# Butterfly weights regrouped between two rounds: trips through DRAM replaced by TensorE transposes, in a decoder block on one Trainium2 core

## The chip, the core and the metric

The kernel runs on one core of a Trainium2 chip (trn2). The metric is the device time of one execution in microseconds (us). TensorE (PE in the profile) multiplies matrices and writes into PSUM; VectorE (DVE), ScalarE (ACT) and GpSimd (POOL) do the element-wise work and empty PSUM; SyncE (SP) issues the DMA transfers. All data are fp32, and every fp32 matmul appears in the trace as two records; a transpose appears as one.

## The reference

Input x has 4 tokens, 2048 batch positions and 512 features. Three residual steps follow one another, each behind a layer norm: a diagonal state-space recurrence along the tokens, a cross-attention with 16 heads over 77 context rows, and a feed-forward net whose hidden layer of 2048 passes through butterfly transforms.

```python
x = x + recurrence(layernorm(x))
x = x + cross_attention(layernorm(x), ctx)
h = layernorm(x) @ W_exp + b_exp              # 512 -> 2048
h = butterfly(h, up_weights)                  # 11 stages
h = gelu(h + up_bias)
h = butterfly(h, down_weights)                # 11 stages
x = x + (h @ W_con + b_con) + down_bias       # 2048 -> 512

def butterfly(y, weights):                    # stage s mixes i with i + 2**s
    for s in range(11):
        yr = y.reshape(*lead, nb, 2, 2 ** s)
        a, b = yr[..., 0, :], yr[..., 1, :]
        w = weights[s]                        # a 2x2 matrix for each pair
        y = stack([w00 * a + w01 * b, w10 * a + w11 * b])
```

## The kernel before, in words

The rows of x are worked in 16 units, each of 128 positions with their 4 tokens. For a unit, `front` does the recurrence, the attention and the last layer norm, and `feed_forward` the rest. `feed_forward` of unit u runs interleaved with `front` of unit u + 1: after every few matmuls, its `step` takes one piece of the other's work. Dense products are done with seven half-size products instead of eight (`seven`, `up`, `down`), so the weights are needed in seven pieces: `up7`, `wq7` and `dn7` in DRAM, `wo` in SBUF.

The butterflies are linear, so an opening (`_prepare`) multiplies them into W_exp and W_con once, on the chip, and the units use dense weights. The 11 stages go in two rounds. The low 7 stages mix only inside blocks of 128 rows: 16 blocks, each a full 128 x 128 matrix `e`, made by `_low_products` from the coefficients (`low_up`, `low_dn`, 2 MB each) in six element-wise steps, each twice as long as the one before. The high 4 stages mix rows that are 128 apart. With the rows regrouped, so that row 16p + m lies on partition p in group m, they are 16 matrices of 128 x 128 in which only 16 diagonals are filled; `diagonal` spreads the products `hp` over a mask to make one such `bd`.

Between the rounds the weights must change from the one order of rows to the other:

- Up: 16 matmuls L258 (512 columns), evictions L230 (ACT) and L232 (DVE) in turn, 16 stores to `rows_up`, four loads back in the other order, then 64 matmuls L283 (128 columns) with `bd`. The bias goes the same way by L259, `brow` and L284.
- Down: 16 matmuls L314 with `bd`, 16 stores to `rows_dn`, four loads back, then 16 matmuls L325 with `e`.

`bd` is made on POOL (L236), as are both sets of low products (L174). SP issues its transfers one after the other; one that stands behind a transfer that must wait waits too.

The opening of the program as a whole: `_recurrence_taps` computes the recurrence's matrices (L111 to L124); `_keys_values` makes keys and values of the context (L147, L156), from tiles that lie in the room of `wup`; then `front(0)` (normalizing L428 and transposes L439, recurrence L469, layer norm L375 to L401 with transposes L410, queries L454, scores L512, softmax L516 to L522, transposed scores L534, outputs L544, output projection L454 with `sw`/`ot`) is taken in turn with the pieces of `_prepare`, one piece of the one for one of the other. Sums of weight blocks (L301 to L304 for up7, L334 to L341 for dn7) come at the end of each half. PSUM banks for `_prepare` rotate among three tags (`banks`). The scheduler orders the instructions of each engine; the first matmul of unit 0's feed-forward is the first L613.

Of the kernel before, what the change touches and what calls it, by code (L numbers as in the profile page):

```python
# [17 lines left out]
P = 128  # L18
# [115 lines left out]
def _keys_values(nc, psum, ctx_t, wk_t, wv_t, kbd, vsb, room):  # L134


    wk = room[:, 0, :].rearrange("p (c e) -> p c e", c=NC)
    wv = room[:, 1, :].rearrange("p (c e) -> p c e", c=NC)
    ct = room[:, 2, 0 : NC * T * NK].rearrange("p (c k) -> p c k", c=NC)
# [3 lines left out]
    nc.gpsimd.memset(kbd, 0.0)  # L143
# [9 lines left out]
    for b in range(T):  # L153
        ps = psum.tile([P, 512], F32, tag="b", name="ps_v")
        for c in range(NC):
            nc.tensor.matmul(ps[0:NK, :], lhsT=ct[:, c, b * NK : (b + 1) * NK], rhs=wv[:, c, :],  # L156
                             start=c == 0, stop=c == NC - 1)
        nc.scalar.copy(vsb[:, b, :], ps[0:NK, :])


def _low_products(nc, low, transposed):


    e, off = low[:, 0 : 2 * NB], 2 * NB
    for s in range(1, LOW):
        n = 2 ** s
        w = low[:, off : off + NB * 2 * n]
        off += NB * 2 * n
        if transposed:
            v, old = w.rearrange("p (x c) -> p x c", c=2), e.unsqueeze(2).to_broadcast([P, NB * n, 2])  # L170
        else:
            v = w.rearrange("p (b r x) -> p b r x", b=NB, r=2)
            old = e.rearrange("p (b x) -> p b x", b=NB).unsqueeze(2).to_broadcast([P, NB, 2, n])
        nc.gpsimd.tensor_tensor(v, v, old, ALU.mult)  # L174
        e = w
    return e.rearrange("p (b x) -> p b x", b=NB)
# [28 lines left out]
def _regrouped(nc, pool, scratch, e, name):  # L205

    nc.sync.dma_start(out=scratch.rearrange("(b j) k -> j b k", j=P), in_=e)
    out = pool.tile([P, NB, NB], F32, tag="hp", bufs=2, name=name)
    nc.sync.dma_start(out=out, in_=scratch.rearrange("(p m) k -> p m k", m=NB))
    return out  # L210


def _prepare(nc, pool, banks, dram, ident, wexp_t, up_low, up_high, up_bias, dn_low, dn_high, wcon, wup, wdn, bias,
# [4 lines left out]

    sub = P // NB
    rows = dram.tile([HID, D], F32, name="rows_up")  # L220
    rows_dn = dram.tile([HID, D], F32, name="rows_dn")
    brow = dram.tile([2, HID], F32, name="brow")
    hscr = [dram.tile([HID, NB], F32, name=f"hscr{i}") for i in range(2)]
    t = wdn
    mask = pool.tile([P, sub], F32, name="mask")
    nc.vector.tensor_reduce(mask, ident.rearrange("p (b i) -> p i b", i=sub), AX.X, ALU.add)

    def evict(i, out, ps):
        if i % 2:
            nc.scalar.copy(out, ps)  # L230
        else:
            nc.vector.tensor_copy(out, ps)  # L232

    def diagonal(hp, m):
        bd = pool.tile([P, NB, sub], F32, tag="bd", bufs=3, name="bd")
        nc.gpsimd.tensor_tensor(bd, hp[:, m, :].unsqueeze(2).to_broadcast([P, NB, sub]),  # L236
                                mask.unsqueeze(1).to_broadcast([P, NB, sub]), ALU.mult)
        return bd.rearrange("p b i -> p (b i)")

    low = pool.tile([P, NB * 2 * (P - 1)], F32, tag="lowc", name="low_up")  # L240
    high = pool.tile([P, HIGH, NB // 2, 4], F32, tag="highc", bufs=2, name="high_up")
    b1 = pool.tile([P, NB], F32, name="b1")
    b2 = pool.tile([P, NB], F32, name="b2")
    nc.sync.dma_start(out=low, in_=up_low)
    nc.sync.dma_start(out=high, in_=up_high)
    nc.sync.dma_start(out=bias, in_=up_bias)
    src = wexp_t.rearrange("(b p) d -> p b d", p=P)
    nc.sync.dma_start(out=b1, in_=src[:, :, D])
    for i in range(4):
        nc.sync.dma_start(out=t[:, 4 * i : 4 * i + 4, :], in_=src[:, 4 * i : 4 * i + 4, 0:D])  # L250
    yield
    e = _low_products(nc, low, False)
    hp = _regrouped(nc, pool, hscr[0], _high_products(nc, pool, high, False), "hp_up")
    yield
    pb = banks()
    for b in range(NB):
        ps = banks()
        nc.tensor.matmul(ps, lhsT=e[:, b, :], rhs=t[:, b, :], start=True, stop=True)  # L258
        nc.tensor.matmul(pb[:, b : b + 1], lhsT=e[:, b, :], rhs=b1[:, b : b + 1], start=True, stop=True)  # L259
        evict(b, t[:, b, :], ps)  # L260
        nc.sync.dma_start(out=rows[b * P : (b + 1) * P, :], in_=t[:, b, :])
        if b % 4 == 3:
            yield
    nc.vector.tensor_copy(b1, pb[:, 0:NB])
    nc.sync.dma_start(out=brow[0, :].rearrange("(b p) -> p b", p=P), in_=b1)
    nc.sync.dma_start(out=b2, in_=brow[0, :].rearrange("(p m) -> p m", m=NB))
    back = rows.rearrange("(p m) d -> p m d", m=NB)
    for i in range(4):
        nc.sync.dma_start(out=t[:, 4 * i : 4 * i + 4, :], in_=back[:, 4 * i : 4 * i + 4, :])
    high = pool.tile([P, HIGH, NB // 2, 4], F32, tag="highc", bufs=2, name="high_dn")  # L270
    nc.sync.dma_start(out=high, in_=dn_high)
    yield
    hp_dn = _regrouped(nc, pool, hscr[1], _high_products(nc, pool, high, True), "hp_dn")
    low = pool.tile([P, NB * 2 * (P - 1)], F32, tag="lowc", name="low_dn")
    nc.sync.dma_start(out=low, in_=dn_low)
    e = _low_products(nc, low, True)
    yield
    pb = banks()
    for m in range(NB):
        bd = diagonal(hp, m)  # L280
        ps = banks().rearrange("p (c k) -> p c k", c=NC)
        for c in range(NC):
            nc.tensor.matmul(ps[:, c, :], lhsT=t[:, m, c * P : (c + 1) * P], rhs=bd, start=True, stop=True)  # L283
        nc.tensor.matmul(pb[:, m : m + 1], lhsT=bd, rhs=b2[:, m : m + 1], start=True, stop=True)  # L284
        evict(m, wup.rearrange("p c (k m) -> p m c k", m=NB)[:, m], ps)
        if m % 4 == 3:
            yield
    nc.vector.tensor_copy(b2, pb[:, 0:NB])
    nc.sync.dma_start(out=brow[1, :].rearrange("(p m) -> p m", m=NB), in_=b2)
    nc.sync.dma_start(out=b1, in_=brow[1, :].rearrange("(b p) -> p b", p=P))  # L290
    nc.vector.tensor_tensor(bias, b1, bias, ALU.add)
    h, k = HID // 2, NC // 2
    for p in range(NB // 2):
# [4 lines left out]
        for i, a in enumerate((a11, a12, a22)):  # L298
            nc.sync.dma_start(out=up7[p][:, i], in_=a)
        s = pool.tile([P, 4, k, P], F32, tag="s", bufs=1, name="s")  # L300
# [3 lines left out]
        nc.vector.tensor_tensor(s[:, 3], a12, s[:, 1], ALU.subtract)  # L304
        nc.sync.dma_start(out=up7[p][:, 3:7], in_=s)
        if p % 2:
            yield
    src = wcon.rearrange("(p m) d -> p m d", m=NB)
    for i in range(4):
        nc.sync.dma_start(out=t[:, 4 * i : 4 * i + 4, :], in_=src[:, 4 * i : 4 * i + 4, :])  # L310
    yield
    for m in range(NB):
        ps = banks()
        nc.tensor.matmul(ps, lhsT=diagonal(hp_dn, m), rhs=t[:, m, :], start=True, stop=True)  # L314
        evict(m, t[:, m, :], ps)
        nc.sync.dma_start(out=rows_dn.rearrange("(p m) d -> p m d", m=NB)[:, m, :], in_=t[:, m, :])
        if m % 4 == 3:
            yield
    src = rows_dn.rearrange("(b p) d -> p b d", p=P)
    for i in range(4):  # L320
        nc.sync.dma_start(out=t[:, 4 * i : 4 * i + 4, :], in_=src[:, 4 * i : 4 * i + 4, :])
    yield
    for b in range(NB):
        ps = banks()
        nc.tensor.matmul(ps, lhsT=e[:, b, :], rhs=t[:, b, :], start=True, stop=True)  # L325
        evict(b, wdn[:, b, :], ps)
        if b % 4 == 3:
            yield
    h = NB // 2
    b11, b12, b21, b22 = (wdn[:, r * h : r * h + h, c * (D // 2) : (c + 1) * (D // 2)] for r in range(2) for c in range(2))  # L330
    t1, t2, t3, n4 = (wup[:, i, :].rearrange("p (b d) -> p b d", b=h) for i in range(4))
    for i, w in ((0, b11), (1, b21), (2, b22)):
        nc.sync.dma_start(out=dn7[i], in_=w)
    nc.vector.tensor_tensor(t1, b12, b11, ALU.subtract)  # L334
    nc.sync.dma_start(out=dn7[4], in_=t1)
    nc.gpsimd.tensor_tensor(t3, b22, b12, ALU.subtract)
    nc.sync.dma_start(out=dn7[6], in_=t3)
    nc.vector.tensor_tensor(t2, b22, t1, ALU.subtract)
    nc.sync.dma_start(out=dn7[5], in_=t2)
    nc.vector.tensor_tensor(n4, b21, t2, ALU.subtract)  # L340
    nc.sync.dma_start(out=dn7[3], in_=n4)  # L341
# [4 lines left out]
def kernel(ctx: ExitStack, tc: tile.TileContext, x, ctx_t, ssm_vec, ssm_vt, ssm_vinv, wq_t, wk_t, wv_t,  # L346
# [16 lines left out]
    make_identity(nc, ident)  # L363

    def load_x(u):
        xt = (xlast if u % 3 == 2 else xpool).tile([P, T, D], F32, tag=f"xt{u % 3}", name=f"xt{u}")
        nc.sync.dma_start(out=xt, in_=x[:, u * P : (u + 1) * P, :].rearrange("t p d -> p t d"))
# [91 lines left out]
    def front(u, xt, res, wq=None):  # L459
# [18 lines left out]
        if wq is None:  # L478
            wq = work.tile([P, 7, NC // 2, D // 2], F32, tag="pt", bufs=1, name="wq")
            nc.sync.dma_start(out=wq, in_=wq7)  # L480
# [108 lines left out]
    def feed_forward(u, xt, rhs, other):  # L589
# [70 lines left out]
        for p in range(h):  # L660
# [3 lines left out]
            up_mid(p)  # L664
            r, d = xt[:, p // 2, p % 2 * (D // 2) : (p % 2 + 1) * (D // 2)], slice(p % 2 * (D // 2), (p % 2 + 1) * (D // 2))
# [58 lines left out]
    xts = {0: load_x(0)}  # L724
    ready = []
    with tc.tile_pool(name="prep", bufs=1) as pool:
        wup = pool.tile([P, NC, HID], F32, name="wup")
        wdn = pool.tile([P, NB, D], F32, name="wdn")
        _recurrence_taps(nc, pool, psum, ssm_vec, ssm_vt, ssm_vinv, gt)
        prep = _prepare(nc, pool, banks, dram, ident, wexp_t, up_low, up_high, up_bias, dn_low, dn_high, wcon,  # L730
                        wup, wdn, hbias, up7, dn7)
        next(prep)
        _keys_values(nc, psum, ctx_t, wk_t, wv_t, kbd, vsb, wup)
        wq = work.tile([P, 7, NC // 2, D // 2], F32, tag="pt", bufs=1, name="wq")
        src = wq_t.rearrange("(c p) e -> p c e", p=P)
# [104 lines left out]
```

## Time and profile before

| | |
|---|---|
| median of 3 runs | 2663.07 us (2663.07 to 2663.37) |
| profiled execution | 2661.34 us |
| its span | 2659.6 us |
| mean granted TensorE clock | 0.989 of full speed |
| PE, DVE, POOL, ACT busy over the span | 96%, 54%, 36%, 30% |
| first L613 matmul (end of the opening) | 246.58 us after the span's start |
| PE, DVE, POOL, ACT busy in 0 to 246.6 | 176.72, 135.06, 102.84, 47.44 us |
| HBM read, written | 306.00, 41.96 MB |

All views come from one profiled execution, whose time is 1.73 us under the median. An engine's busy time counts its instructions, not what it waits for. A row of groups reads: line, engine, operation, output and inputs, shapes, number of records, then busy time in us, the mean of one record in ns, and the idle time ahead of them with what ended it. A row of the chain gives start and length in us, engine, tile and line. A row of the windows gives the stretch in us, its length, and the busy time of each engine in it.

### The profile page before, as it was taken

To read this page: it belongs to the slowest core of one execution; us is meant where nothing else is said; L and a number is where in the kernel's file an instruction comes from. 1 tells how busy PE (TensorE), PEld (TensorE's weight loads), DVE (VectorE), ACT (ScalarE), POOL (GpSimd) and SP (SyncE) were. 2 spreads that over 40 slices of the span, in tenths; PEclk is the share of its full clock that TensorE was granted. 3 is DMA by queue.
4 is the path that set the end of the run, shared out by engine and by line. 5 is a ranking of instruction groups with operands and counts; after the bars stand their busy time and mean duration, and the time that the engine had idled before them with its cause. 6 is when DMAs were issued, how large, how long until landed. Compare 5 with 4: busy or idle time off the path is not lost.

```text
span 2659.6 us, 36812 instructions
## 1 busy us (share of the span) xinstructions
PE 2565.1 (96%) x14216; PEld 2157.9 (81%) x14216; DVE 1439.1 (54%) x3308; ACT 793.6 (30%) x1440; POOL 965.7 (36%) x1054
## 2 busy tenths in 40 slices
PE   6787999999999999999999999999999999999999
PEld 3545888888888888888888888888888888888888
DVE  4366554565465455546555555645555564554541
ACT  1222413324141332414133341413234241423420
POOL 5343351523334152433415243342524234252523
PEclk9898999999999999999999999999999999999999
DMA  7575233342423334342333333233343324333243
GB/s 265 187 253 210 104 123 124 111 145 97 144 102 131 119 115 137 116 138 93 134 113 127 125 121 133 105 133 107 121 138 112 138 96 145 105 127 108 96 130 139
DMA packets 100158, 350.34 MB, mean 132 GB/s; under 512 B 17936, under 2 KB 46736, under 8 KB 81808
## 3 DMA queue, kind: packets, MB, share of 16 engines
q1 hardware_dynamic: 99984, 347.98, 37.9%
q8 instruction: 113, 1.85, 0.3%
q14 instruction: 61, 0.50, 0.1%
HBM read 306.00 MB, written 41.96 MB: 131 GB/s over the span
## 4 chain that ended last, share of the span: by engine, by line
PE 85%; DVE 6%; ACT 5%; DMA 2%; POOL 1%; issue 1%; SPq 0%; ACTq 0%; DVEq 0%; POOLq 0%
PE ps_a L678 13%; PE ps_b L613 10%; PE ps_b L678 8%; PE ps_w L454 7%; PE ps_q L454 7%; PE ps_c L613 7%; PE ps_a L613 7%; PE ps_c L678 6%; PE ps_sc L512 5%; PE ps_pt L534 4%; PE ps_s L469 3%; PE ps_o L544 2%; PE ps_t L410 2%; ACT L518 1%; ACT L618 1%; DVE st L375 1%
## 5 line engine op out<-in xcount | busy, mean ns | idle before, releaser
L613 PE MATMUL ps_b<-tb,w_up 128*128 128x256 f32 x1536 | 396.7, 379 | 0.0
L678 PE MATMUL ps_a<-w_dn,a 128*128 128x256 f32 x1536 | 373.0, 380 | 0.0
L656 POOL TENSOR_TENSOR s<-a,a 128x256 f32<-128x256 f32 x128 | 93.1, 727 | 675.3 <-ACT a L618 452.8
L613 PEld LDWEIGHTS ps_b<-tb,w_up 128*128 128x128 f32 x1536 | 287.1, 190 | 39.5 <-DVE tb L585 0.4
L678 PEld LDWEIGHTS ps_a<-w_dn,a 128*128 128x128 f32 x1536 | 282.4, 190 | 41.6 <-issue 3.0
L618 ACT ACTIVATE a<-a,hbias 128x256 f32<-128x256 f32 x384 | 193.7, 508 | 408.7 <-DVE a L651 277.6
L613 PE MATMUL ps_a<-xnt,w_up 128*128 128x256 f32 x1024 | 263.9, 380 | 0.0
L678 PE MATMUL ps_c<-w_dn,s 128*128 128x256 f32 x1024 | 248.6, 379 | 0.0
L411 ACT COPY xnt<-ps_t 128x512 f32<-128x512 f32 x128 | 73.6, 587 | 546.5 <-PE ps_t L410 546.5
L522 POOL TENSOR_TENSOR pr<-pr,sm 128x1232 f32<-128x1232 f32 x64 | 144.0, 2249 | 248.7 <-DVE sm L521 242.4
L613 PEld LDWEIGHTS ps_a<-xnt,w_up 128*128 128x128 f32 x1024 | 191.9, 191 | 25.7
L678 PEld LDWEIGHTS ps_c<-w_dn,s 128*128 128x128 f32 x1024 | 188.7, 190 | 27.8
L666 POOL TENSOR_TENSOR xt<-xt,ybias 128x256 f32<-128x256 f32 x128 | 99.9, 813 | 236.9 <-DVE xn L401 236.9
L562 DVE TENSOR_TENSOR xt<-ps_w,xt 128x512 f32<-128x512 f32 x96 | 66.1, 689 | 213.3 <-PE ps_w L454 144.2
L512 PE MATMUL ps_sc<-kbd,qt 128*128 128x308 f32 x512 | 176.6, 442 | 5.1 <-DVE pr L517 3.5
L534 PE MATMUL ps_pt<-ident,pr 128*77 128x128 f32 x1024 | 145.3, 277 | 14.2 <-DVE pt L539 5.7
L534 PEld LDWEIGHTS ps_pt<-ident,pr 128*77 128x77 f32 x1024 | 117.9, 148 | 49.1 <-ACT a L618 11.0
L454 PE MATMUL ps_q<-xnt,wq 128*128 128x256 f32 x640 | 153.2, 382 | 2.1 <-DVE qt L491 1.4
L518 ACT ACTIVATE pr<-pr 128x308 f32<-128x308 f32 x256 | 111.5, 457 | 137.1 <-DVE pr L517 136.6
L454 PEld LDWEIGHTS ps_q<-xnt,wq 128*128 128x128 f32 x640 | 122.1, 191 | 20.2 <-DVE qt L491 1.8
L613 PE MATMUL ps_c<-tb,w_up 128*128 128x256 f32 x512 | 131.7, 379 | 0.4 <-DVE tb L583 0.4
L613 PE MATMUL ps_c<-xnt,w_up 128*128 128x256 f32 x512 | 131.5, 379 | 0.0
(196 smaller groups left out, 4461.6 us busy)
## 6 DMA issues: line engine op xcount, KB each, us to landing
w_up<-up SPq DMA_DIRECT2D x128, 896.0 KB, 4.6
w_dn<-dn SPq DMA_DIRECT2D x112, 1024.0 KB, 4.8
wq<-wq SPq DMA_DIRECT2D x16, 1792.0 KB, 7.6
xt<-in_x SPq DMA_DIRECT2D x16, 1024.0 KB, 5.5
out<-xt SPq DMA_DIRECT2D x64, 256.0 KB, 4.8
wdn<-in_wexp_t SPq DMA_DIRECT2D x4, 1024.0 KB, 10.7
rows_up<-wdn SPq DMA_DIRECT2D x16, 256.0 KB, 2.9
wdn<-rows_up SPq DMA_DIRECT2D x4, 1024.0 KB, 12.5
```

Source lines behind the costliest of these rows:

```text
L411: nc.scalar.copy(xnt[:, :, t, :], ps)
L454: nc.tensor.matmul(tiles[key][:, r, :], lhsT=lhs(i, r, k), rhs=rhs(i, r, k), start=key == i and r == 0 and k == 0, stop=k == 1, skip_group ...
L469: nc.tensor.matmul(ps[:, 2 * i : T, f * NS : (f + 1) * NS], lhsT=xpt[:, i, c * (P // NS) + f, :], rhs=gt[:, 0 : T - 2 * i, :], start=i == ...
L512: nc.tensor.matmul(ps[:, 0 : 4 * NK], lhsT=qt[:, g, t, :], rhs=kbd[:, t, g, :], start=True, stop=True)
L518: nc.scalar.activation(pg, pg, AF.Exp, scale=1.0 / math.sqrt(DH))
L522: nc.gpsimd.tensor_tensor(pr, pr, sm.unsqueeze(2).to_broadcast([P, NH, NK]), ALU.mult)
L534: nc.tensor.transpose(pt_ps[0:NK, j, :], pr[:, 4 * g + j, :], ident)
L613: nc.tensor.matmul(ps, lhsT=w[:, c, :], rhs=rhs[i - 1][:, c], start=first and c == 0, stop=c == 1, skip_group_check=True)
L618: nc.scalar.activation(out, x, AF.Gelu, bias=hbias[:, b : b + 1])
L656: nc.gpsimd.tensor_tensor(s1, a21, a22, ALU.add)
L666: nc.gpsimd.tensor_tensor(r, r, ybias[:, d], ALU.add)
L678: nc.tensor.matmul(ps[:, t, :], lhsT=act[p][lhs[i]][:, t, :], rhs=w[:, p, :], start=first and p == 0 and t == 0, stop=p == h - 1, skip_gro ...
```

## The change

What it does, in the changed file's lines:

- *Up.* The first round is turned over: 64 matmuls L276 of 128 columns with `wdn` (that is, w_exp) as the stationary operand and `e` as the moving one, so that the features lie on partitions. The evictions write them into `mid` (the room of `wup`), grouped by m. 64 transposes L285, four to an eviction, bring group m to `t`. Then 64 matmuls L298 with `bd`: four groups m share a PSUM bank, each writing every fourth column.
- *Down.* The second round comes first as before, as 64 matmuls L333 in the same manner as L298, then 64 transposes L343, then 16 matmuls L352 with `e`, in an order that lets the stores of `dn7` go in two halves.
- `bd` is made on DVE. Evictions go 3 to ACT and 2 to DVE of every five. The last of the low_up products is shared by DVE and POOL, and its load is in two parts. The bias matmuls L267 come ahead of the others. `s` has two buffers.
- The order: coefficients and w_exp are loaded first, x after them; the keys and values come behind the up weights, from tiles of their own; the products of low_dn come after the sums of the up weights; `ybias` is summed at the very end; the load of x for unit u + 2 comes after the second p in `feed_forward`. Some instructions are held to the program's order (`keep_in_program_order`, `keep`).

The core of the diff of `_prepare`:

```diff
-    for b in range(NB):
-        ps = banks()
-        nc.tensor.matmul(ps, lhsT=e[:, b, :], rhs=t[:, b, :], start=True, stop=True)
-        nc.tensor.matmul(pb[:, b : b + 1], lhsT=e[:, b, :], rhs=b1[:, b : b + 1], start=True, stop=True)
-        evict(b, t[:, b, :], ps)
-        nc.sync.dma_start(out=rows[b * P : (b + 1) * P, :], in_=t[:, b, :])
...
-    back = rows.rearrange("(p m) d -> p m d", m=NB)
-    for i in range(4):
-        nc.sync.dma_start(out=t[:, 4 * i : 4 * i + 4, :], in_=back[:, 4 * i : 4 * i + 4, :])
...
+    mid = wup.rearrange("p c (m k) -> p c m k", m=NB)
+    for g in range(4):
+        for c in range(NC):
+            ps = banks()
+            for j in range(4):
+                b = 4 * g + j
+                nc.tensor.matmul(ps[:, j * P : (j + 1) * P], lhsT=t[:, b, c * P : (c + 1) * P],      # L276
+                                 rhs=e[:, b, :], start=j == 0, stop=True, skip_group_check=True)
+            evict(mid[:, c, :, 32 * g : 32 * g + 32].rearrange("p m k -> p k m"), ps.rearrange("p (k m) -> p k m", m=NB))
...
+    for m in range(NB):
+        ps = banks()
+        for c in range(NC):
+            nc.tensor.transpose(ps[:, c * P : (c + 1) * P], mid[:, c, m, :], ident)                  # L285
+        evict(t[:, m, :], ps)
...
+    for g in range(4):
+        bd = [diagonal(hp, 4 * g + j) for j in range(4)]
+        for c in range(NC):
+            ps = banks()
+            for j in range(4):
+                nc.tensor.matmul(ps.rearrange("p (k m) -> p m k", m=4)[:, j], lhsT=t[:, 4 * g + j, c * P : (c + 1) * P],  # L298
+                                 rhs=bd[j], start=j == 0, stop=True, skip_group_check=True)
+            evict(wup[:, c, :].rearrange("p (k m) -> p k m", m=NB)[:, :, 4 * g : 4 * g + 4], ps.rearrange("p (k m) -> p k m", m=4))
...
-        nc.sync.dma_start(out=rows_dn.rearrange("(p m) d -> p m d", m=NB)[:, m, :], in_=t[:, m, :])
...
+    def turned(b):
+        ps = banks()
+        for c in range(NC):
+            nc.tensor.transpose(ps[:, c * P : (c + 1) * P], wup[:, c, b * P : (b + 1) * P], ident)  # L343
+        evict(t[:, b, :], ps)
```

In the whole program, `prep` is taken five pieces ahead of `front(0)`, and the weights of the queries are loaded after its first pieces:

```diff
-        for _ in prep:
-            next(first, None)
+        for _ in range(5):
+            next(prep)
...
+        for n, _ in enumerate(prep):
+            for _ in range(1 + (n > 8)):
+                next(first, None)
+            if n == 7:
+                next(keys)
```

## The prediction

> **What bounds the kernel now.** I read the busy windows first, then the chain of waits, then the groups by shape. The columns of the windows are stretch, length, busy time of PE, weight loads, DVE, ACT and POOL (instruction records in brackets), granted PE clock, DMA share, GB/s.
>
> ```profile
> 0.00:246.60 246.60, 176.72 (x809) 114.17 (x810) 135.06 (x312) 47.44 (x77) 102.84 (x161) 0.89 0.71 243
> 400.00:550.00 150.00, 148.67 (x847) 127.01 (x847) 83.74 (x197) 48.41 (x88) 53.62 (x56) 1.00 0.34 118
> 84.00:90.74 6.74, 0.06 (x2) 0.01 (x1) 6.16 (x24) 0.00 (x0) 0.00 (x0) 0.83 0.82 190
> 90.74:94.35 3.61, 3.61 (x17) 3.00 (x17) 1.49 (x3) 1.76 (x3) 0.00 (x0) 0.50 0.90 53
> 154.61:219.65 65.04, 49.44 (x266) 26.00 (x267) 49.45 (x75) 17.74 (x34) 22.11 (x14) 0.86 0.79 294
> ```
>
> After the opening TensorE is busy for 148.67 of 150 us, so nothing but TensorE work counts there. The opening ends at 246.58, with the first L613 matmul of unit 0; in it PE is idle for about 70 us. In the built programs the PE rows from that matmul on are the same one by one, and so are ACT's; DVE, POOL and SP differ by the bias add and the x load only. So the opening alone can change the time. What it waits for stands in the chain (start, length, who):
>
> ```profile
> 3.16 8.62 DMA low_up<-in_up_low
> ...
> 22.20 4.46 POOL low_up L174
> 26.70 2.08 PE ps_p L258 x2
> ...
> 57.52 13.73 PE ps_v L156 x32
> ...
> 88.03 17.89 DMA low_dn<-in_dn_low
> ...
> 181.62 3.13 DMA rows_dn<-wdn
> ...
> 185.35 9.40 DMA wdn<-rows_dn
> ...
> 194.80 10.57 PE ps_p L325 x24
> ```
>
> Two DRAM trips stand in it. The up weights are stored, and their reload keeps the queue full (DMA share 0.90) while low_dn comes in; the down weights are stored and reloaded between 181.62 and 194.80, 13.2 us. One matmul of 512 columns is two records, so L156 gives 13.73 / 16 = 0.858 at full clock, and 0.2145 for 128 columns.
>
> ```profile
> L283 PE MATMUL ps_p<-bd,wdn 128*128 128x128 f32 x128 | 18.3, 295 | 0.0
> L232 DVE COPY wdn<-ps_p 128x512 f32<-128x512 f32 x24 | 16.3, 687 | 34.4 <-PE ps_p L258 26.7 <-PE ps_p L325 4.1 <-PE ps_p L314 3.4
> L230 ACT COPY wdn<-ps_p 128x512 f32<-128x512 f32 x24 | 14.1, 586 | 47.1 <-PE ps_p L258 27.0 <-PE ps_p L314 10.7 <-PE ps_p L325 9.4
> L232 DVE COPY wup<-ps_p 128x512 f32<-128x512 f32 x8 | 8.3, 1037 | 12.8 <-PE ps_p L283 12.8
> ```
>
> A contiguous eviction takes 0.69 on DVE and 0.59 on ACT; one whose writes are 64 bytes apart, 1.04 on DVE (its ACT twin 1.035).
>
> **The change step by step.** New lines are those of the changed file. Each step gets the time at which it ends.
>
> *First round.* The load of low_up is split, so the six products on POOL start with the first half, and the longest, 4.46 on POOL, is shared: half of it is 2.3 on POOL. low_up lands at 11.8 before; half of its 2 MB, first in the queue, should be there near 7. The products before the last sum to 0.32 + 0.45 + 0.73 + 1.22 + 2.29 = 5.0, and the high products no longer sit among them (3.15 + 1.49 + 0.56 = 5.2 out of the path). So the matmuls start at 7 + 5.0 + 2.3, some 15 instead of 26.7 (bounds 13, and 20 if the second half or w_exp lands late). The 16 one-column bias matmuls L267 now stand ahead, partly at low clock: 5.5, to 20.5. The same work as before, now 64 matmuls L276, 64 x 0.2145 = 13.7, with about 4 of recurrence among them: 38.4. Its 16 strided evictions, 16 x 1.04 on two engines = 8.3, hide beside it.
>
> *Transposes of the up weights.* 64 of L285 replace the trip. In the 3.61 us row 16 of them took 0.226 each at clock 0.50, so 0.113 at full clock: 7.2 of PE. Sixteen evictions, 7 x 0.69 on DVE and 9 x 0.59 on ACT, lie beside the normalizing of unit 0 (L428, 0.71 each, on DVE), so evictions set the stage: 9.8 with it, 1.4 for the eviction ahead and 0.7 for the first diagonal block: 50.3.
>
> A rule speaks against these stretches: the Trainium skill, TensorE: Matmul & The Clock Gate, section Part 4: PE-mode transpose, says that transposes do not count as busy for the clock gate. Its row here shows 0.50, but after 6.7 us with nothing on PE, which leaves rule and idleness apart as causes. If the clock stayed at 0.50 through a stretch, 64 x 0.226 = 14.5 would replace 9.8; I take 3 us for both stretches together (bounds 0 and 6.4, the clock row on either side).
>
> *Second round, up.* The 64 matmuls L298 are those of L283, 18.3 there; recurrence sums 3.3 and waits behind DVE, which shares a lock with POOL's wq products, 2.4: 74.3. That such a lock is there: a DVE subtraction of 2048 columns took 2.28 alone and 5.99 while POOL did one, which took 6.97. Diagonal blocks leave POOL, 32 x 0.43, for DVE, where an operation twice as wide took 0.42; I take 0.26. Waiting in that place for brow (9.9 before, PE behind a 7.0 us load) goes: b2 is fetched under the transposes.
>
> *Keys, values.* 8.55 + 13.73 in the chain plus 1.3 of L498: 97.8. Beside them lie the sums s and the up7 stores, which cost some 5.5 us each pair in the chain before (3.28 of it a store that the single s buffer waited on); with two buffers I take 3 each, 8 in 23 us, done with the matmuls. Were that cover gone, it would cost up to 5.
>
> *Statistics.* Before, PE stood 6.7 us (84.00 to 90.74) while DVE did the layer norm of unit 0; that stays, 7.6 with 0.9 of eviction: 105.4. Then 16 transposes cold, 3.6, and the first queries, 8.7: 117.7.
>
> *Down weights.* On POOL the products of low_dn (10 us) now stand behind s and before the query sums; the first four diagonal blocks share DVE with them, 4.3: 122. The remaining queries and three groups of L333 take 18.3: 140.3. Then attention and L343, L352. DVE carries it: maxima 7.6, subtractions 7.5, sums 5.7 + 1.0, transposed scores out 5.4, outputs 2.8, blocks 1.1, evictions 10, t1, t2, n4 as halves 6.9 = 48.0; 8 for the lock and 5 for waits on PE give 61, to 201.3 (bounds 50 and 70; the stage from 154.61 to 219.65 was 65.0 with 49.45 on DVE and both trips' end in it).
>
> *Tail.* From the last attention output 27.4 before (219.65 to 246.58 and its issue). The eight additions L666 on POOL, 0.79 each, leave this place; beside them the last Newton steps took 0.65 instead of 0.2, so 2.4 go: 25, to 226.3. SP also carries fourteen half stores of dn7 instead of seven, but they start with the first half, some 15 us earlier; a store lands in 5 and w_up in 4.6, by about 219. A new wait: the fourth operand n4 of unit 0 stands on POOL behind the bias add, which waits for the down-bias load; ready 5.8 after the first L613 and needed at 9.4. If that cover went, the excess is paid once. The load of wq at the start of a unit and that of x two units on are in new places on SP; w_up passes both, and wq has 38.4 - 19.5 - 7.6 = 11.3 us to spare (issue, landing and first use within a unit).
>
> *Sum.* 246.6 - 226.3 = 20.3, less 3 for the clock: 17.3. Profiled time: 2661.3 - 17.3 = 2644.0 (its span of 2659.6 and 1.7 around it). The median of the runs lies 1.7 above the profiled execution, so 2663.1 - 17.3 = 2645.8, rounded to 2646.
>
> **Rivals.** *Strided writes into PSUM slow TensorE.* L298 and L333, 128 matmuls, write every fourth column. No row of before does that: the nearest, L469, writes blocks of 64 columns and runs at 0.43 for 256, the contiguous rate. As L283 goes at 0.2145 when warm, writes that double it add 128 x 0.2145 = 27.5, and the kernel is 10 slower, 2673. It decides from 17.3 / 128 = 0.135 more for each matmul. Below zero it can't go, since the columns are the same. I take nothing, the nearest row's value. The Trainium skill, Advanced Engine Details and Errata, section Memory Cachelines, speaks for it: any PSUM pattern that isn't contiguous slows matmuls significantly. It gives no figure; no row here agrees or differs yet.
>
> *One wait for another.* The fixed order lets PE stand at POOL's low_dn products, the statistics and SP's stores for as long as it stood at the trips: the last stage at its 70 and 8 more at the blocks, gain about 0 (-5 to 5), 2663. For it: DVE and POOL are as full as before in the stage from 154.61, 49.45 of 65. Against it: the trip of 13.2 is in the chain, and no work takes its place.
>
> *The early start counts in full.* With the late stage at 50 instead of 61, the gain is 28 to 33, 2632. Against it: 48.0 of DVE work leaves 2 us for all waits.
>
> That the change doesn't do what it says is excluded: the built program has 128 more transposes and no row stores.
>
> **How the numbers follow.** A measurement here tells 0.2%, 5.3 us. Forecast, a gain of 5.3 to 31: 0.74; over 31: 0.08; about nothing: 0.08, of which 0.07 within 5.3; strided writes, slower by over 5.3: 0.10. Slower comes to 0.11, faster to 0.82. The unknown ends of the steps add as squares, 5, 4, 9 and 2.4 one way, 11 and 2 the other: gain 6 to 28. Reaching for eight in ten across the cases I take a gain of 1 to 33: 2630 to 2662, which holds the forecast's 0.74 and some 0.07 of its neighbours.
>
> **What would show it.** In the profile after: the first L276 near 15 to 20 us; L298 and L333 near 18 us for 128 records (36 would be the rival); the stretch of L285 near 10 at a clock above 0.8; PE waiting about 7 for DVE at the statistics; the first L613 at 226 to 230; and windows past it unchanged at 148.67 of 150. A first L613 beyond 245, or a steady window with less PE, makes the prediction wrong.

## The result and the profile after

The changed kernel takes 2661.61 us (median of 12 runs, 2659.90 to 2666.95), the kernel before 2663.07 (12 runs, 2660.91 to 2664.74). The ratio is 0.9997, 95% interval 0.9989 to 1.0006: no change, where 2646 was forecast.

The profiled execution took 2664.3 us, 2.7 above the median of its kernel and 3.0 above the one before. Its windows, with the columns of before (stretch, length, busy time of PE, weight loads, DVE, ACT, POOL, granted PE clock, DMA share, GB/s):

```profile
0.00:248.90 248.90, 195.05 (x1128) 152.99 (x1129) 157.71 (x352) 61.62 (x103) 81.28 (x122) 0.93 0.51 165
400.00:550.00 150.00, 148.67 (x846) 127.00 (x845) 82.36 (x195) 47.79 (x87) 53.34 (x56) 1.00 0.35 125
20.80:47.60 26.80, 26.77 (x111) 23.17 (x111) 6.08 (x18) 3.51 (x4) 11.51 (x64) 1.00 0.79 201
160.46:217.97 57.51, 50.49 (x354) 33.68 (x352) 47.80 (x76) 24.32 (x47) 13.93 (x6) 0.94 0.22 78
```

The steady part is as it was, 148.67 of 150. The first L613 of before (the matmul is L642 now) starts at 248.96 instead of 246.58, so 2.4 of the 2.9 us by which this execution's span is longer lie in the opening. PE is idle there for 53.9 us instead of 69.9, since the trips are gone, but it is busy for 18 us more: new work, and old work done slowly. The third row is the surprise: PE is idle for only 0.03 of 26.8 us, and yet the first round is late. The timeline of PE over it and behind (start, length, line, tile, records, idle time ahead):

```profile
20.83 6.99 PE L267 MATMUL ps_p<-b,low_up 128*128 128x1 f32 x32 [1.57 <-DVE low_up L179]
...
42.90 2.93 PE L276 MATMUL ps_p<-low_up,wdn 128*128 128x128 f32 x12
...
47.91 8.75 PE L276 MATMUL ps_p<-low_up,wdn 128*128 128x128 f32 x76
...
57.54 5.24 PE L285 MATMUL ps_p<-ident,wup 128*128 128x128 f32 x46 [0.65 <-DVE w L415]
```

Twelve records in 2.93 us are 0.244 each, 76 in 8.75 are 0.115: until 47.6 the same instruction runs at half rate. The window's clock of 1.00 doesn't show it; the durations have to be read instead. In before, TensorE came up from half rate within 4 us of the first matmul of 512 columns:

```profile
26.70 2.08 PE L258 MATMUL ps_p<-wdn,low_up 128*128 128x512 f32 x2 [4.73 <-POOL low_up L174]
...
29.32 1.65 PE L258 MATMUL ps_p<-wdn,low_up 128*128 128x512 f32 x2
...
32.52 1.13 PE L258 MATMUL ps_p<-wdn,low_up 128*128 128x512 f32 x2
```

The width alone doesn't explain that. In the run with both trips below, the same matmuls of 512 columns stand in the place of L276, with the same small matmuls of the recurrence among them, and needed about 12 us:

```profile
20.78 2.08 PE L270 MATMUL ps_p<-wdn,low_up 128*128 128x512 f32 x2 [1.57 <-DVE low_up L179]
...
32.24 1.64 PE L270 MATMUL ps_p<-wdn,low_up 128*128 128x512 f32 x2
...
34.75 1.13 PE L270 MATMUL ps_p<-wdn,low_up 128*128 128x512 f32 x2
```

The round also starts late. Ahead of it, from the timeline of all engines:

```profile
8.21 7.78 POOL L179 TENSOR_TENSOR low_up<-low_up 128x64 f32<-128x64 f32 x6 [2.53 <-DMA low_up<-in_up_low]
...
13.81 2.93 DVE L62 SCALAR_TENSOR_TENSOR exp_p<-exp_p,exp_r 64x1 f32<-64x1 f32 x5
...
19.30 0.34 DVE L127 TENSOR_SCALAR ti<-ps_ri,az 64x128 f32<-64x128 f32 x1 [1.27 <-PE ps_ri L124]
19.57 1.21 DVE L179 TENSOR_TENSOR low_up<-low_up 128x1024 f32<-128x1024 f32 x1
```

The second place is the start of the down round. The timeline of three engines:

```profile
132.19 9.38 POOL L179 TENSOR_TENSOR low_dn<-low_dn 128x64 f32<-128x64 f32 x6
...
135.04 6.68 DVE L242 TENSOR_TENSOR bd<-hp_dn,mask 128x128 f32<-128x128 f32 x4
...
141.77 4.79 PE L333 MATMUL ps_p<-bd,wdn 128*128 128x128 f32 x26 [3.55 <-DVE bd L242]
...
148.94 0.89 DVE L242 TENSOR_TENSOR bd<-hp_dn,mask 128x128 f32<-128x128 f32 x4
```

Four diagonal blocks take DVE 0.89 us alone and 6.68 beside POOL's products. Last, the groups by shape that answer to L283:

```profile
L333 PE MATMUL ps_p<-bd,wdn 128*128 128x128 f32 x128 | 20.1, 325 | 7.6 <-DVE bd L242 7.6
L298 PE MATMUL ps_p<-bd,wdn 128*128 128x128 f32 x128 | 15.4, 277 | 0.1
```

L298, which writes every fourth column, has a mean of 277 ns against 295 for L283 of before. L333 writes the same way; its mean of 325 holds records at half rate behind PE's waits, and 32 of it in one piece took 3.73 us (at 149.43), 0.117 each.

The stages side by side, end times in us:

| stage | forecast end (length) | after, end (length) | difference |
|---|---|---|---|
| start of the first round | 15.0 | 20.8 | +5.8 |
| first round: L267 and L276 | 38.4 (23.4) | 56.5 (35.7) | +12.3 |
| transposes L285 | 50.3 (11.9) | 66.7 (10.2) | -1.7 |
| L298 | 74.3 (24.0) | 89.3 (22.6) | -1.4 |
| keys, values | 97.8 (23.5) | 112.6 (23.3) | -0.2 |
| statistics | 105.4 (7.6) | 121.1 (8.5) | +0.9 |
| first queries, first down blocks | 122.0 (16.6) | 141.8 (20.7) | +4.1 |
| queries, three groups of L333 | 140.3 (18.3) | 160.5 (18.7) | +0.4 |
| attention and down weights | 201.3 (61.0) | 221.7 (61.2) | +0.2 |
| tail | 226.3 (25.0) | 249.0 (27.3) | +2.3 |

Of the 22.7 us, 18.1 stand in the first two rows and 4.1 at the blocks. This execution is 2.7 us above the median, and its first round is a long one: in the profiles of four runs below that leave the round as it is (the products ahead, the down weights through DRAM, both of these, the blocks on GpSimd), it took 31.2 to 32.2 us.

### The profile page after: what moved, and what is told of

The parts are those of the page before. It is cut to its first block, busy times and chain, and to the rows that moved or that the text cites. A ratio compares the mean times of both kernels' runs of the same rounds, so it can differ in the third digit from the quotient of the medians.

```text
span 2662.5 us, 37405 instructions
## 1 busy us (share of the span) xinstructions
PE 2583.4 (97%) x14536; PEld 2196.8 (83%) x14536; DVE 1463.9 (55%) x3350; ACT 807.3 (30%) x1466; POOL 949.9 (36%) x1023
## 3 DMA queue, kind: packets, MB, share of 16 engines
q1 hardware_dynamic: 94480, 331.21, 35.7%
## 4 chain that ended last, share of the span: by engine, by line
PE 86%; DVE 7%; ACT 5%; issue 2%; POOL 0%; DMA 0%; SPq 0%; ACTq 0%; DVEq 0%; POOLq 0%
PE ps_a L709 13%; PE ps_b L642 10%; PE ps_b L709 8%; PE ps_q L483 7%; PE ps_w L483 7%; PE ps_c L642 7%; PE ps_a L642 7%; PE ps_c L709 6%; PE ps_sc L541 5%; PE ps_pt L563 4%; PE ps_s L498 3%; PE ps_o L573 2%; PE ps_t L439 2%; ACT L547 1%; ACT L647 1%
## 5 line engine op out<-in xcount | busy, mean ns | idle before, releaser
L642 PE MATMUL ps_b<-tb,w_up 128*128 128x256 f32 x1536 | 396.8, 379 | 1.2 <-DVE u L659 1.2
L642 PEld LDWEIGHTS ps_b<-tb,w_up 128*128 128x128 f32 x1536 | 287.0, 190 | 40.9 <-issue 1.6
L642 PE MATMUL ps_a<-xnt,w_up 128*128 128x256 f32 x1024 | 263.9, 381 | 0.0
L642 PEld LDWEIGHTS ps_a<-xnt,w_up 128*128 128x128 f32 x1024 | 192.0, 191 | 25.7
L483 PE MATMUL ps_q<-xnt,wq 128*128 128x256 f32 x640 | 152.4, 381 | 0.7 <-ACT qt L523 0.7
L547 ACT ACTIVATE pr<-pr 128x308 f32<-128x308 f32 x256 | 111.5, 457 | 118.5 <-DVE pr L546 117.9
L483 PEld LDWEIGHTS ps_q<-xnt,wq 128*128 128x128 f32 x640 | 122.1, 191 | 17.9 <-ACT qt L523 1.1
L642 PE MATMUL ps_c<-tb,w_up 128*128 128x256 f32 x512 | 131.6, 379 | 0.0
L642 PE MATMUL ps_c<-xnt,w_up 128*128 128x256 f32 x512 | 131.5, 379 | 0.0
```

Source lines behind the costliest of these rows:

```text
L483: nc.tensor.matmul(tiles[key][:, r, :], lhsT=lhs(i, r, k), rhs=rhs(i, r, k), start=key == i and r == 0 and k == 0, stop=k == 1, skip_group ...
L547: nc.scalar.activation(pg, pg, AF.Exp, scale=1.0 / math.sqrt(DH))
L642: nc.tensor.matmul(ps, lhsT=w[:, c, :], rhs=rhs[i - 1][:, c], start=first and c == 0, stop=c == 1, skip_group_check=True)
```

## The experiments

All are the changed kernel with the edit shown or named; its line numbers shift by a few in them. Times are medians, ratios are to the kernel before. "Layer norm to end" is the stretch in the profile from the first layer-norm transpose L439 to the first up matmul L642: 155.8 us before, 127.9 after. Before, the second round of the up weights lies in it; after, it lies ahead. Each is read from one profile: in three runs whose code from there on is the changed kernel's (the bias matmuls behind L276, the first round warm with GpSimd's order held, the same with the bias in parts), it is 129.0, 122.0 and 120.5.

**Seven unused matmuls ahead of the first round.**

```diff
+        ps = psum.tile([P, 512], F32, tag="a", name="ps_warm")
+        for _ in range(7):
+            nc.tensor.matmul(ps.rearrange("p (j k) -> p j k", j=4), lhsT=ident, rhs=ident.unsqueeze(1).to_broadcast([P, 4, P]), ...)
```

> Edit: the changed kernel with seven matmuls of 512 columns (identity by identity, results unused) on TensorE ahead of L123, where it stood idle from 10.5 to 18.2 us. Theory A (the clock: TensorE ran at half rate from 20.8 to 47.6 us although it was never idle, and that took 13 us): the clock is granted before the first L276, the first round ends at 43 to 46 us instead of 56.5, the first L642 comes at 236 to 239 instead of 249.0, and the kernel takes 10 to 13 us less than the changed kernel, some 2649 to 2652. Rival B (the half rate comes from DMA traffic or from POOL's and DVE's access to SBUF in that stretch): L276 stays at 0.48 us each until about 47, no gain, 2660 to 2663. Rival C (a later stage is bound by transfers or by POOL, so that what is gained early is given back): the first round ends by 46, but the first L642 stays within 3 us of 249.

2651.41 us, ratio 0.9957 (0.9946 to 0.9969). The first round falls from 35.8 to 25.7 us, so most of its excess was the clock. A full DMA queue was not the cause: behind L267 the rate fell to half with the queue as full as before (19.40 to 22.90: DMA share 1.05, granted clock 1.00; 23.00 to 26.50: 1.06 and 0.53). But GpSimd's order changed too: the scheduler moved the products of `wo` and low_dn up beside the diagonal blocks of the up round, four of which then took 5.43 us on DVE. L298 lasted 33.5 instead of 22.6 and gave that gain back, while the blocks of the down round were free and layer norm to end was 115.4. The run mixes two causes.

**The same, with GpSimd's order held.**

```diff
-                nc.gpsimd.tensor_tensor(wo[:, 4], wo[:, 6], wo[:, 0], ALU.subtract)
+                tc.keep_in_program_order(nc.gpsimd.tensor_tensor(wo[:, 4], wo[:, 6], wo[:, 0], ALU.subtract))
```

> Edit: the seven matmuls of 512 columns ahead of L123 once more, and the first product of wo held behind what stands ahead of it on POOL, so that POOL's order is the changed kernel's (with the seven matmuls alone the products of wo and low_dn had moved ahead of the sums s, into the second round of the up weights). This leaves the clock of the first round as the only difference. Theory A: the first round ends near 45 instead of 56.5, what follows keeps its lengths, and the first L642 comes at 237 to 241; the kernel takes 6 to 12 us less than the changed kernel. Rival C: the second round of the up weights then waits for POOL's wq products or the diagonal blocks and gives back most of it: first L642 at 245 or later, gain under 4.

2649.30, ratio 0.9948 (0.9935 to 0.9961). L298 is back at 23.6. But the clock was not held; the timeline of PE:

```profile
18.77 0.43 PE L123 MATMUL ps_ri<-pz,vt 64*64 64x128 f32 x2
...
19.37 4.99 PE L267 MATMUL ps_p<-b,low_up 128*128 128x1 f32 x32
24.22 2.48 PE L276 MATMUL ps_p<-low_up,wdn 128*128 128x128 f32 x10
```

L123 takes 0.43, full rate, ahead of the one-column matmuls L267; after them ten records take 2.48, half rate, and so on to 35.2; from 24.20 to 35.00 the granted clock is 0.50. PE was never idle in between.

**The bias matmuls behind L276 instead of ahead of it.**

> Edit: the changed kernel with the sixteen one-column bias matmuls L267 (7.0 us at half rate) behind the 64 matmuls L276 instead of ahead of them. Theory A, in the form that one-column matmuls do not bring the clock up: L276 starts at 20.8 instead of 27.7 and the clock is granted earlier by about as much, near 40; the first round and the bias end at 48 to 52 instead of 56.5, the gain is 4 to 8 us. Theory A', the recurrence matmuls between the L276 keep the clock down and the bias matmuls don't matter: the clock is granted at 46 to 48 as before, gain 3 to 4 us (the bias matmuls then run at full rate). Rival B: gain 0 to 1.

2662.36, ratio 0.9998 (0.9986 to 1.0009), with runs from 2653.69 to 2670.63, the widest of all: as a cure it failed. In its profile (2668.87 us, one of the slow ones) full rate came 11 us after the first L276, but the one-column stretch took the clock away at its new place:

```profile
45.69 4.71 PE L278 MATMUL ps_p<-b,low_up 128*128 128x1 f32 x32
50.27 7.66 PE L285 MATMUL ps_p<-ident,wup 128*128 128x128 f32 x48
```

48 transposes in 7.66 us, where the changed kernel did 46 in 5.24; from 50.30 to 54.00 the granted clock is 0.50.

**The bias matmuls in four parts, one behind each group of L276, on top of the warm start.**

```diff
+        for b in range(4 * g, 4 * g + 4):
+            nc.tensor.matmul(pb[:, b : b + 1], lhsT=e[:, b, :], rhs=b1[:, b : b + 1], start=True, stop=True)
```

> Edit: the changed kernel with the seven unused matmuls ahead of L123, POOL's order held, and the sixteen one-column bias matmuls spread, four behind each group of sixteen L276, as L303 stands behind L298. In the last runs the seven matmuls brought the clock up by 15 us, but behind the 7 us of one-column matmuls it stood at half again for 3.4, 13.7 and 20.5 us. Theory A' (a stretch with one-column or small matmuls reads as idle to the clock, and how long it stays down is chance): the clock now stays full through the first round, which ends at 40 to 43; the first L642 comes at 229 to 234, and the runs spread less than the changed kernel's 7 us; 2642 to 2647. Rival: the recurrence matmuls between the L276 bring it down by themselves: end at 46 to 52, first L642 at 236 or later, 2649 to 2655.

2651.07, ratio 0.9955 (0.9942 to 0.9967). The first round now takes 25.7 us in the place of the 30.4 of the run with GpSimd's order held, and yet the time is no better: PE waits 2.4 for brow, its mean clock over the stage is 0.88, L298's stage lasts 28.2 instead of 23.6, and the wait at the statistics grows from 8.4 to 10.0. What was won ahead was gone behind the next waits.

**The products of low_dn moved ahead, between the sums of the up weights.**

```diff
+        if p == 2:
+            e = _low_products(nc, keep, low, True, False)
...
-    e = _low_products(nc, keep, low, True, False)
```

> Edit: the changed kernel with POOL's six low_dn products put between the second and the third pair of sums s (near 97 to 107 us, under keys and values) instead of behind the fourth product of wo (132 to 141.6). Theory: the four diagonal blocks at 135.0 took 6.7 us because DVE shared a lock with these products, and PE waited 4.6 us in that place; the blocks then take 1 us and the first L642 comes 4 to 6 us earlier, if the sums s and the up7 stores, now 9 us later, stay hidden. Rival: the products delay the sums and the stores, the statistics or the queries wait for them, and the gain is 0 or a loss of up to 5.

2653.29, ratio 0.9956 (0.9942 to 0.9970). The products run at 87 to 97 beside keys and values. In the timeline four blocks take 0.89 at once and the first group of L333 runs in one piece at full rate:

```profile
129.32 0.89 DVE L242 TENSOR_TENSOR bd<-hp_dn,mask 128x128 f32<-128x128 f32 x4
...
129.75 3.74 PE L334 MATMUL ps_p<-bd,wdn 128*128 128x128 f32 x32
```

Layer norm to end falls from 127.9 to 115.4. Between the two runs with a warm start and GpSimd's order held, without and with this move, it falls from 122.0 to 114.7. So a meeting that the forecast priced at 4.3 cost 7 to 12.5 us. Not only the 6.68 on DVE is in it: behind PE's wait the granted clock is 0.59 (141.77 to 144.00). How the rest divides is not shown.

**The diagonal blocks back on GpSimd.**

```diff
-        keep(nc.vector.tensor_tensor(bd, hp[:, m, :].unsqueeze(2).to_broadcast([P, NB, sub]),
+        keep(nc.gpsimd.tensor_tensor(bd, hp[:, m, :].unsqueeze(2).to_broadcast([P, NB, sub]),
```

> The changed kernel with one part undone: all diagonal blocks are made on GpSimd again, as in the kernel before. Theory (VectorE's blocks are slow in the down round because GpSimd's low_dn products hold the lock that both engines share, so what is lost there is the meeting of the two): on GpSimd the first four down blocks stand directly behind the products that end at 141.6, so they are ready near 143 and the first group of L333 comes no earlier than the 141.8 of the changed kernel; the later groups wait for GpSimd behind its own work at 168, VectorE's 1.1 us of blocks go out of its chain. The stretch from the first layer-norm transposes to the first up matmul stays within 124 to 131 (127.9 in the changed kernel, 115.4 where the products were moved away), and the time within 4 us of the changed kernel's. Rival (the fault is that the blocks were given to VectorE, the engine that carries the attention): the stretch falls by 6 us or more, to 122 or less, and the time with it.

2659.50, ratio 0.9981 (0.9972 to 0.9990). Layer norm to end is 127.1, within the theory's bounds. The first blocks queue behind the products:

```profile
127.45 9.12 POOL L179 TENSOR_TENSOR low_dn<-low_dn 128x64 f32<-128x64 f32 x6
136.53 1.49 POOL L242 TENSOR_TENSOR bd<-hp_dn,mask 128x128 f32<-128x128 f32 x4
...
136.99 5.54 PE L333 MATMUL ps_p<-bd,wdn 128*128 128x128 f32 x32 [4.66 <-POOL bd L242]
```

So the engine was not at fault, the products' place was: on one engine the blocks wait for them, on the other they share the lock with them.

**The down weights through DRAM again** (16 matmuls of 512 columns with `bd`, 16 stores, 4 loads, no L343).

```diff
-        bd = [diagonal(hp_dn, 4 * g + j) for j in range(4)]
...
+        for m in range(4 * g, 4 * g + 4):
             ps = banks()
+            nc.tensor.matmul(ps, lhsT=diagonal(hp_dn, m), rhs=t[:, m, :], start=True, stop=True)
+            evict(t[:, m, :], ps)
+            nc.sync.dma_start(out=rows_dn.rearrange("(p m) d -> p m d", m=NB)[:, m, :], in_=t[:, m, :])
+    for i in (0, 2, 1, 3):
+        nc.sync.dma_start(out=t[:, 4 * i : 4 * i + 4, :], in_=src[:, 4 * i : 4 * i + 4, :])
```

> Edit: one part of the change undone: the down weights go through DRAM again (16 matmuls of 512 columns with the diagonal blocks, 16 stores, four loads, 16 matmuls with e), the up weights stay on the chip. The prediction's step (the trip of 13.2 us stood in the chain, and no work took its place): slower than the changed kernel by 8 to 13 us. Rival D (the attention of unit 0, bound by DVE, covers the trip anyway, and the 64 transposes with their 16 evictions cost as much): within 3 us of the changed kernel or up to 5 faster.

2654.19, ratio 0.9960 (0.9946 to 0.9973). The trip that the change removed makes the changed kernel faster when it is put back: layer norm to end 115.4.

**Down weights through DRAM, and low_dn's products ahead.**

> Edit: the down weights through DRAM, with POOL's low_dn products between the second and third pair of sums. Compared with the same early products and the transposes on chip (first L643 at 232.7, from the first L440 transpose 115.4 us). Theory D (attention hides the trip; what the change lost in this place was the diagonal blocks, which share a lock with the low_dn products): within 2 us of that kernel in the stretch from the first L431 transpose to the first L634 matmul (113 to 117). The prediction's step (the trip lies on the path): that stretch is 8 to 13 us longer, 123 to 128.

2647.00, ratio 0.9931 (0.9919 to 0.9942). Layer norm to end 108.9, 6.5 less than with the transposes in the same order; the medians of the two runs differ by 6.3 (2653.29 and 2647.00). The attention's stretch, from the first score to the first output projection, in the windows of the run with the products ahead and of this one:

```profile
147.38:202.29 54.91, 47.90 (x354) 31.07 (x352) 47.80 (x76) 24.33 (x47) 13.92 (x6) 1.00 0.23 82
```

```profile
145.19:196.41 51.22, 43.94 (x271) 23.32 (x269) 41.53 (x74) 20.42 (x39) 11.86 (x6) 1.00 0.58 212
160.50:168.90 8.40, 6.43 (x57) 3.66 (x55) 6.74 (x13) 3.43 (x8) 2.25 (x1) 1.00 0.66 225
```

With the trip DVE, the engine that carries the stage, has 6.3 us less to do in it and PE 4.0: DVE empties 10 banks there instead of 15 (6.7 us for 10.3 in their rows), and its blocks and sums of weight blocks take less time too. The trip does stand in the chain of this run:

```profile
161.34 2.01 DMA rows_dn<-wdn
163.37 5.50 DMA wdn<-rows_dn
```

But over these 8.4 us PE is busy for 6.43 and DVE for 6.74 (the second window row): the attention is worked there, and would have to be worked after it otherwise.

**Both trips, in the new order, with low_dn's products ahead and keys and values moved into the up weights' trip.**

> Edit: the changed kernel's order with low_dn early, but both trips through DRAM again: the first round of the up weights as 16 matmuls of 512 columns with 16 stores and four loads, and keys and values (22 us of TensorE) moved into that wait; no weight transposes at all. Theory D' (a trip costs nothing when TensorE has other work in that place, and the transposes with their evictions cost TensorE time that the trip doesn't): first up matmul at 214 to 222, against 226.2 with the up weights on chip; 2634 to 2642. The prediction's view (the trips are what the opening waits for): 234 to 242, 2655 to 2663.

2644.57, ratio 0.9929 (0.9917 to 0.9942). No weight is transposed, and the kernel is 17.0 faster than the changed one and equal, within the intervals, to the run with the down trip alone. The 512-column matmuls are back in the first round, and keys and values fill 51.4 to 73.9 while the weights are away.

**Warm start and low_dn's products ahead.**

> Edit: both remedies on the changed kernel, the seven matmuls ahead of L123 and the early low_dn products, with POOL's order held. If the two losses are separate, the gains add: first round's end near 45 and 115.4 us from the first transpose of the layer norm to the first up matmul, which then comes at 225 to 228; some 2643 to 2646 us. If they are one and the same slack, it stays at 232 to 233 and 2650 to 2653.

2652.29, ratio 0.9956 (0.9940 to 0.9972). Not the sum of the two: the first round again went cold behind L267 (its end at 53.5 against 49.8), and the statistics waited 11.1 instead of 8.5. Layer norm to end is 114.7.

**The same with seven unused matmuls in each of unit 0's layer norms, to hold the clock there.**

> Edit: the kernel of both remedies, and seven more unused matmuls of 512 columns on TensorE in each of the two waits of unit 0 for the layer norm (7.2 and 7.8 us), which depend on the last residual sum. Theory A: the clock does not fall to half there, so the 16 transposes after each take 1.8 instead of 3.6 us and the first matmuls behind them run at full rate: 4 to 7 us less than the kernel of both remedies. Rival: DVE's layer norm is slowed by TensorE's reading of the same tile, or the evictions set the pace of the transposes: under 2 us.

2652.47, ratio 0.9951 (0.9939 to 0.9963): nothing. The transposes after the last layer norm ran at full rate, 1.8 us ahead of the first up matmul where 3.6 stood, yet layer norm to end is 116.9. What took the gain back at these two places is not shown.

**Warm start, bias in four parts, low_dn's products ahead, down weights through DRAM.**

> Edit: up weights on chip, down weights through DRAM, low_dn early, and the first round with the seven matmuls and the spread bias matmuls. Theory A' and D together: the first round ends at 40 to 43 instead of 52.3, the rest of the opening keeps its lengths, first up matmul at 214 to 219; 2634 to 2640. Rival C (what starts earlier waits for the wq loads, the diagonal blocks or the statistics): 222 to 226, 2642 to 2647.

2641.10, ratio 0.9913 (0.9900 to 0.9927), faster than both kernels. The timeline of PE, full rate from the first record to the end of the round:

```profile
19.43 1.60 PE L273 MATMUL ps_p<-low_up,wdn 128*128 128x128 f32 x12
...
38.90 3.82 PE L273 MATMUL ps_p<-low_up,wdn 128*128 128x128 f32 x32
42.55 0.95 PE L277 MATMUL ps_b<-b,low_up 128*128 128x1 f32 x8
```

The first round takes 24.1 us, the forecast's 23.4 and what it assumed: full clock. Layer norm to end is 111.5. Against the run without the warm start and the bias in parts, which ends the round at 52.3 instead of 43.5, little of this is left in the profile at the first layer-norm transposes (116.0 and 117.3) and nothing at the first up matmul (227.5 and 226.2); but this profile is of the run's slowest execution and that one of its fastest; the medians differ by 5.9 us, with intervals that overlap. So the round was slow because of the clock, but how much of the opening a fast round is worth in the end is open.

## Why the prediction was wrong

- **The step that failed is the first round.** Its 64 x 0.2145 is a price at full clock, and only the bias matmuls were thought "partly at low clock". In the profile before the same work (L258) had taken 19.0 us, partly at half rate, and not 13.7. After, TensorE ran at half rate for 26.8 us, and the stage took 35.7 instead of 23.4 (31.2 to 32.2 in four other profiles). The bounds for the clock (0 to 6.4) stood on the transposes and not here, so no term and no rival held it. That 2661.61 lies just inside 2630 to 2662 is luck: the range was wide for other terms. Shown: held at full clock, the round takes 24.1.
- **The start, 15 (bounds 13 and 20), was 20.8.** The first half of low_up was there at 8.2 and GpSimd's products took 7.78 for 5.0 + 2.3; that gives 16. The half of the last product that went to DVE ran at 19.57 only, in program order behind L127 (19.30), which waits for PE's L123 of 18.18. A term priced as "half of it" had moved into another queue, and what is queued there was left out. That queue was late itself: five small instructions L62 took DVE 2.93 us and one took 2.30 beside GpSimd's products, where six of them took 1.09 ahead of the products. Read from the trace, not tried on its own.
- **The down blocks, 4.3 for the lock, were mis-sized.** The wait was named; the stage with it took 4.1 more than forecast, and moving the products away was worth 7 to 12.5 in all. The place of the products decides, not the engine of the blocks.
- **The trip of 13.2 in the chain was not a price.** The sum rebuilt the late stage from DVE's work, and rightly gave it 61 (61.2 measured). What it didn't do was to price the stage with the trip kept. In the same order the trip is 6.5 us better than the transposes, for the chain's DMA rows lie beside attention that must be worked anyway. "No work takes its place" in the second rival's "against" is the sentence that the runs refute.
- **Where the gain went.** PE waits for 16.0 us less in the opening and works for 18.3 more. The weight transposes are 17.6 of that work (L285 7.54, L343 10.03), and the first round with its bias matmuls takes 28.9 us of PE instead of 23.2. That is not the rival's one wait for another: the time is its 2663, by another mechanism. Layer norm to end is 28 us shorter and what is ahead of it 30 longer (the first layer-norm transposes start at 121.1 instead of 90.7), but this is mostly work that changed sides: the up weights' transposes and second round, 32.8 us (56.5 to 89.3), now run ahead of them, where L283 of before ran behind them (113.6 to 131.9).
- **What held.** L298's stage 22.6 for 24.0, the transposes 10.2 for 11.9, keys and values 23.3 for 23.5, attention 61.2 for 61.0 (in part luck: DVE was busy for 51.5 us of it, not 48.0), an unchanged steady part. The tail missed by 2.3: the Newton steps are shorter, as forecast (from the first normalizing L430 to L642 4.25, from L401 to L613 before 6.0), but PE waits 3.2 for `sw` on DVE ahead of L483, whose next eight records then take 3.75 instead of 1.9.
- **Strided writes into PSUM** cost nothing: 277 ns for L298 against 295 for L283, which writes contiguously. The Trainium skill, Advanced Engine Details and Errata, section Memory Cachelines, which says otherwise, is not borne out for fp32 writes of TensorE 16 bytes apart.
- **The transposes and the clock.** After 7.2 us of idle time 16 transposes ran at half rate, and the full clock was granted just behind them (mean 0.90 over the next 2 us); in the profiles of two other runs the rate rose before the last of the 16 (3.39 and 3.46 us):

```profile
121.07:124.68 3.61, 3.61 (x16) 3.00 (x17) 1.49 (x3) 1.76 (x3) 0.00 (x0) 0.50 0.96 275
```

The 46 of L285 above ran at 0.114 each throughout. So the rule that I weighed (the Trainium skill, TensorE: Matmul & The Clock Gate, section Part 4: PE-mode transpose) doesn't hold here. The 3 us taken for it were not paid; the clock was lost one step earlier.

Open: how the clock weighs small matmuls, and what the recurrence's matmuls between the others do to it. Full rate came at 47.6 in the profile of the changed kernel, and at 36.7 to 39.0 in those of the four runs with the same first round, so a single profile can be 10 us from another here; the changed kernel's runs spread over 7 us and those of before over 4. No run with both sets of weights on the chip cures the start, the first round and the down blocks without a new loss elsewhere; that these terms make up the whole miss is read from the stage table of one profile. The comparison of up weights by trip and by transposes (2644.57 and 2647.00) mixes the trip with the place of keys and values.

## What to carry to other kernels

A matmul's price holds only at the clock of its place: at the head of a program, ask from when TensorE runs at full rate, and read the rate from durations. A transfer in the chain is no price; ask what the engine that carries the stage does meanwhile, and what the replacement adds to it. Two engines under one lock want their work in different stages, and moving half an instruction to another engine puts it at the end of that engine's queue.

## What the runs showed of the hardware

- TensorE without a gap can stay at half rate: 26.8 us in the changed kernel, on 32 one-column records followed by 128-column ones mixed with 64-row matmuls of the recurrence. From the first L276 it took 9 to 11 us in four other profiles, 11 without the one-column matmuls ahead, and about 12 with 512 columns in the place of the 128, so the width did not decide. The seven unused matmuls of 512 columns, with nothing between them, took 7.52 to 9.10 us for 14 records in six profiles; from 0.429 a record at full rate I estimate 3 to 6 us at half rate. The Trainium skill, TensorE: Matmul & The Clock Gate, section Part 1: The HAM clock gate (the "warmup" mystery), calls the warm-up some 3.4 us of time, not a number of matmuls. Here what is issued in that time counts as well.
- Behind a run of one-column matmuls the full clock was gone: 32 records in 3.7 to 5.0 us in all five profiles in which it was up ahead of them, and 18 in 2.17 us in the run with both trips (granted clock 0.55 from 43.20 to 46.80). In groups of eight in the first round it was gone in one profile of two.
- A VectorE instruction of 128 columns beside GpSimd's element-wise products took 6.68 / 4 = 1.67 us in the mean instead of 0.89 / 4 = 0.22.
